# Second mlp of a hybrid block: table rows and layer-norm output transposed in 32x32 blocks by VectorE and placed through DRAM

## The chip, the cores and the metric

The kernel runs on one core of a Trainium2 chip. The metric is the device time of one execution in microseconds (us); a kernel's time is the median of its runs. One execution was also recorded by the hardware profiler. Its span runs from the first to the last recorded event, and line numbers such as L1442 are lines of the kernel before the change.

## The reference

The input is `x`, 4 x 1024 tokens of 256 floats. Four blocks are added one after the other, each on a layer norm of `x`: a state-space block, an mlp with experts, an attention block, and the same mlp with experts once more. The change lies in this last one. With `h` the layer norm of `x`, as rows (all in fp32):

```python
queries = (h @ W_q).reshape(2, n, 64)
routing = einsum('tnd,tdk->tnk', queries, keys)       # 64 scores per half
# the best 8 of each half, their 64 sums, the best 8 of those: 8 indices below 512 (clamped)
ew = silu(einsum('nh,nkh->nk', h, down_embed[indices])) * softmax(scores)
experts = einsum('nk,nkh->nh', ew, up_embed[indices])
x = x + silu(h @ gate_w) * (h @ up_w) @ down_w + experts
```

`reshape(2, n, 64)` makes the scores of one token come from two far apart places, so the scores of a group of tokens need `h` of a group in the first half and of one in the second.

## The kernel before

The 4096 tokens are cut into 8 groups of 512, each held as 4 tiles of 128 tokens. In `ffn` (L1663 on), the second mlp, everything for a group `g` goes this way.

First, for all groups in the order 0, 4, 1, 5, 2, 6, 3, 7 (that of the attention's results), `layernorm` writes ln(x) with tokens on partitions (L111), TensorE transposes it in 128x128 blocks against an identity (`transposed`, L120), and VectorE and ScalarE each copy one half of the result out of PSUM into `hT[g]`, features on partitions (L1681).

Then `route` turns two `hT` into a table: 128 partitions x 4 x 512 floats, `tb`, in which every token has its expert weights at the places of its experts and zero elsewhere. It is a chain of some forty VectorE operations (L1300 to L1435); ScalarE fills in entries (L1360). The scores for table `g` need `hT[g//2]` and `hT[g//2+4]`. The table of group `g+1` is made while group `g` is finished.

For each group in rising order: 8 pairs of gate and up products (`product`, L129) with silu on ScalarE (L1699) and a product on VectorE (`act`, L1701); `chosen` multiplies `hT` by all 512 rows of `down_emb`, takes silu (`wt`, L1454) and weighs it with the table; the scores for the next table; `raise_x` adds down products of `act` and `up_emb` products of `wt` for four tiles, and VectorE adds each to `x` (L1473); `store` writes the group out (L1711).

The table has tokens on partitions and `wt` has experts there, so `spread` has TensorE transpose it, 4 x 4 blocks of 128x128 into `st` in PSUM (L1442), and VectorE multiplies `wt` by each `st` (L1458).

```python
for i in range(4):
    st = self.spread(stp, table, i)
    nc.vector.tensor_tensor(
        wv[:, :, i // 2, :, i % 2], wv[:, :, i // 2, :, i % 2], st, ALU.mult
    )
```

Earlier stages record every operation at L46 and are kept in the order written by hand. In `ffn` the framework's scheduler orders the instructions of each engine when the program is built; that order is fixed in the program. An engine works through its own queue in order, and an instruction that waits holds up all behind it. SP's queue issues nearly all DMAs. The buffers of a pool are reused in turn, and whoever writes one waits for its last reader. DMAs signal on eight semaphores in turn, and each waits for the one that used its semaphore before.

Of the kernel before, what the change touches and what calls it, by code (L numbers as in the profile page):

```python
# [12 lines left out]
F32 = mybir.dt.float32  # L13
AF = mybir.ActivationFunctionType
ALU = mybir.AluOpType
AX = mybir.AxisListType
PSUM = bass.MemoryType.PSUM
DRAM = bass.MemoryType.DRAM

P = 128  # L20
B, L, D = 4, 1024, 256
NT = B * L
KD = D // P
G = 512
NG = NT // G
TG = G // P
# [3 lines left out]
XC = NEXP // P  # L30
# [20 lines left out]
class Net:  # L51
# [1383 lines left out]
        dve.tensor_tensor(tb[:, :, NEXP - 1], tb[:, :, NEXP - 1], last, ALU.add)  # L1435
        got.append(tb)

    def spread(self, pool, tb, i):

        st = pool.tile([P, XC, P], F32, tag="st", name="st")  # L1440
        for c in range(XC):
            self.nc.tensor.transpose(st[:, c, :], tb[:, i, c * P : (c + 1) * P], self.ident)  # L1442
        return st

    def chosen(self, pool, stp, mm, w, h, table):

        nc = self.nc
        wt = pool.tile([P, XC, G], F32, tag="wt", name="wt")
        for c in range(XC):
            ps = self.product(  # L1450
                mm,
                [(w["down_embT"][:, k, c * P : (c + 1) * P], h[:, k, :]) for k in range(KD)],
            )
            nc.scalar.activation(wt[:, c, :], ps, AF.Silu)  # L1454
        wv = wt.rearrange("p c (m j h) -> p c m j h", h=2, j=P)
        for i in range(4):
            st = self.spread(stp, table, i)
            nc.vector.tensor_tensor(  # L1458
                wv[:, :, i // 2, :, i % 2], wv[:, :, i // 2, :, i % 2], st, ALU.mult
            )  # L1460
        return wt

    def raise_x(self, pool, g, w, wt, act):
# [199 lines left out]
    def ffn(self, w, out):  # L1663
        nc, tc = self.nc, self.tc
        with ExitStack() as ctx:
            one = ctx.enter_context(tc.tile_pool(name="ff_one", bufs=1, reuse_waits="tile"))
            two = ctx.enter_context(tc.tile_pool(name="ff_two", bufs=2, reuse_waits="tile"))
            sm = ctx.enter_context(tc.tile_pool(name="ff_sm", bufs=2, reuse_waits="tile"))
            acts = ctx.enter_context(tc.tile_pool(name="ff_act", bufs=IC + 2, reuse_waits="tile"))
            mm = ctx.enter_context(tc.tile_pool(name="ff_mm", bufs=4, space=PSUM, reuse_waits="tile"))  # L1670
            stp = ctx.enter_context(tc.tile_pool(name="ff_st", bufs=2, space=PSUM, reuse_waits="tile"))
            op = ctx.enter_context(tc.tile_pool(name="ff_o", bufs=2, space=PSUM, reuse_waits="tile"))

            hT = [None] * NG
            for g in (0, 4, 1, 5, 2, 6, 3, 7):
                h = one.tile([P, KD, G], F32, tag=f"hT{g}", name=f"hT{g}")
                ln = two.tile([P, TG, D], F32, tag="ln", name="ln")
                self.layernorm(g, ln)
                for k in range(KD):
                    ps = self.transposed(mm, ln, k)  # L1680
                    (nc.scalar.copy if k else nc.vector.tensor_copy)(h[:, k, :], ps)  # L1681
                hT[g] = h

            def route(g):
                got = []
                for _ in self.route(nc, w, g, hT, (one, two, sm, mm), got):
                    pass
                return got[0]

            table = route(0)  # L1690
            for g in range(NG):
                h = hT[g]
                act = []
                for c in range(IC):
                    cs = slice(c * P, (c + 1) * P)
                    pg = self.product(mm, [(w["gate_w"][:, k, cs], h[:, k, :]) for k in range(KD)])
                    pu = self.product(mm, [(w["up_w"][:, k, cs], h[:, k, :]) for k in range(KD)])
                    s = two.tile([P, G], F32, tag="s", name="s")
                    nc.scalar.activation(s, pg, AF.Silu)  # L1699
                    a = acts.tile([P, G], F32, tag="act", name="act")  # L1700
                    nc.vector.tensor_tensor(a, s, pu, ALU.mult)  # L1701
                    act.append(a)
                wt = self.chosen(two, stp, mm, w, h, table)
                if g + 1 < NG:
                    table = route(g + 1)
                self.raise_x(op, g, w, wt, act)
                self.store(out, g)
# [73 lines left out]
```

## Time and profile before

| what | value |
|---|---|
| median of 3 runs | 2012.34 us (2011.7 to 2013.0) |
| profiled execution, its own time | 2012.48 us |
| its span | 2010.8 us, 22729 instructions |
| mean granted clock of TensorE | 0.96 |
| busy: TensorE, VectorE, ScalarE, GpSimd | 89%, 79%, 57%, 44% |
| second mlp: first product L129 with `w_gate_w` | about 1528 us |
| DMA, mean over the span | 48 GB/s; in the second mlp about 10 GB/s |

A busy share is an average over stages with different limits, so the second mlp is read by itself, in stretches that follow its groups. A group line gives line, engine, operation, output<-input, count, busy us and mean ns. SPq lines are the DMA issues on SP's queue; "to landing" is the time from an issue until its completion is signalled.

### The profile page before, as it was taken

The numbers are of one execution on the slowest core, as the hardware profiler recorded it, in microseconds if no ns is written. First come the engines' busy times: TensorE is split into PE (matmuls) and PEld (weight loads), VectorE is DVE, ScalarE is ACT, GpSimd is POOL, SyncE is SP. The second block draws the span as 40 slices with busy tenths as digits, with TensorE's granted clock in tenths as the row PEclk, the third lists the DMA queues.
The fourth block names the chain that finished last, engine by engine and source line by source line (L and its number), as shares of the span: only waits on it lengthen the run. The fifth ranks groups of instructions, "written<-read, shape, count | busy, mean of one in ns | idle before, by whom it ended". The sixth has DMA issues, their size and how long they took to land.

```text
span 2010.8 us, 22729 instructions
## 1 busy us (share of the span) xinstructions
PE 1789.5 (89%) x7450; PEld 1145.2 (57%) x7450; DVE 1592.4 (79%) x2695; ACT 1137.7 (57%) x2315; POOL 894.2 (44%) x612
## 2 busy tenths in 40 slices
PE   8777789889798898898878998899988999999999
PEld 4445446456455564564645656566664666556665
DVE  6999999999999999999999999654457555445551
ACT  5877777867787677776543654745324333233331
POOL 4977888878798797887760000111110000000000
PEclk8868899999999999999899999899998999999999
DMA  4111121221212212212123131010000000000000
GB/s 138 53 33 58 54 73 48 88 73 57 82 56 79 70 53 80 74 59 64 56 81 116 63 100 46 34 63 1 1 1 0 11 11 1 11 11 11 11 11 11
DMA packets 79926, 97.46 MB, mean 48 GB/s; under 512 B 7360, under 2 KB 53312, under 8 KB 79808
## 3 DMA queue, kind: packets, MB, share of 16 engines
q1 hardware_dynamic: 74592, 90.66, 14.6%
q10 hardware_dynamic: 5216, 5.36, 0.8%
q8 instruction: 58, 0.95, 0.2%
q14 instruction: 60, 0.49, 0.1%
HBM read 83.15 MB, written 12.85 MB: 48 GB/s over the span
## 4 chain that ended last, share of the span: by engine, by line
PE 50%; DVE 30%; ACT 11%; issue 8%; POOL 1%; DMA 0%; DVEq 0%; SPq 0%; POOLq 0%; ACTq 0%
PE ps L129 22%; DVE h L46 9%; DVE acc L46 8%; PE hT L46 4%; ACT a L46 3%; PE down L46 3%; PE o L46 2%; PE up L46 2%; PE gate L46 2%; PE skip L46 2%; PE out L46 1%; PE dt L46 1%; PE at L46 1%; ACT xc L46 1%; PE bc L46 1%
## 5 line engine op out<-in xcount | busy, mean ns | idle before, releaser
L46 POOL TENSOR_TENSOR u<-dx,bt 128x1024 f32<-128x1024 f32 x255 | 602.0, 2362 | 140.4 <-DVE h L46 106.0
L46 ACT ACTIVATE a<-delta,a_neg 128x512 f32<-128x512 f32 x512 | 340.9, 687 | 147.9 <-DVE h L46 146.8
L46 PE MATMUL hT<-ident,h 128*128 128x128 f32 x2048 | 317.1, 294 | 120.2 <-DVE acc L46 119.1
L46 PEld LDWEIGHTS hT<-ident,h 128*128 128x128 f32 x2048 | 245.4, 149 | 265.5 <-DVE acc L46 228.4
L46 DVE SCALAR_TENSOR_TENSOR acc<-hT,cT,acc 128x512 f32<-128x512 f32 x512 | 356.8, 740 | 18.0 <-PE hT L46 17.4
L46 DVE TENSOR_TENSOR_SCAN h<-a,state,u 128x512 f32<-128x512 f32 x256 | 317.8, 1285 | 1.3 <-ACT a L46 1.2
L46 DVE TENSOR_TENSOR_SCAN h<-a,u 128x512 f32<-128x512 f32 x256 | 303.9, 1232 | 4.8 <-ACT a L46 2.6
L1701 DVE TENSOR_TENSOR act<-s,ps 128x512 f32<-128x512 f32 x64 | 44.0, 688 | 151.4 <-PE ps L129 151.3
L46 PE MATMUL gate<-hT,gate_w 128*128 128x512 f32 x256 | 124.9, 611 | 14.3 <-ACT acc L46 14.3
L1699 ACT ACTIVATE s<-ps 128x512 f32<-128x512 f32 x64 | 38.1, 596 | 167.4 <-PE ps L129 164.6
L46 PE MATMUL up<-hT,up_w 128*128 128x512 f32 x256 | 122.0, 599 | 2.9 <-DVE xw L46 2.9
L129 PE MATMUL ps<-hT,w_gate_w 128*128 128x512 f32 x256 | 122.1, 600 | 2.5 <-DVE act L1701 2.5
L46 POOL TENSOR_TENSOR xc<-xc,tap 128x512 f32<-128x512 f32 x84 | 110.9, 1320 | 22.8 <-ACT tap L46 22.6
L129 PE MATMUL ps<-hT,w_up_w 128*128 128x512 f32 x256 | 120.3, 592 | 0.0
L46 PE MATMUL down<-w_down_w,av 128*128 128x256 f32 x512 | 118.6, 380 | 1.8 <-DVE xw L46 1.0
L129 PE MATMUL ps<-w_down_w,act 128*128 128x256 f32 x512 | 116.8, 380 | 3.0 <-DVE x L1473 3.0
L129 PEld LDWEIGHTS ps<-w_down_w,act 128*128 128x128 f32 x512 | 96.0, 190 | 21.6 <-DVE x L1473 8.8
L46 PEld LDWEIGHTS down<-w_down_w,av 128*128 128x128 f32 x512 | 94.9, 190 | 20.6 <-issue 8.0
L1360 ACT ACTIVATE tb<-d,ex 128x64 f32<-128x64 f32 x256 | 62.0, 333 | 53.4 <-DVE ex L1350 48.4
L46 ACT ACT_TABLE_LOAD x63 | 80.8, 1283 | 17.7 <-DMA w_wd2T<-in_wd2T 8.8
L46 PE MATMUL out<-w_out_wT,y 128*128 128x256 f32 x256 | 68.3, 414 | 18.6 <-DVE y L46 18.4
L129 PEld LDWEIGHTS ps<-hT,w_gate_w 128*128 128x128 f32 x256 | 48.9, 192 | 60.4 <-issue 56.0
(296 smaller groups left out, 3079.0 us busy)
## 6 DMA issues: line engine op xcount, KB each, us to landing
bt<-bcd SPq DMA_DIRECT2D x127, 256.0 KB, 3.2
gate_w<-in_gate_w SPq DMA_DIRECT2D x64, 128.0 KB, 2.5
up_w<-in_up_w SPq DMA_DIRECT2D x64, 128.0 KB, 2.2
in_wT<-in_in_wT SPq DMA_DIRECT2D x8, 512.0 KB, 3.8
hs<-hT SPq DMA_DIRECT2D x8, 512.0 KB, 2.9
xs<-xw SPq DMA_DIRECT2D x8, 512.0 KB, 2.8
hT<-hs SPq DMA_DIRECT2D x8, 512.0 KB, 4.5
x<-xs SPq DMA_DIRECT2D x8, 512.0 KB, 4.6
```

Source lines behind the costliest of these rows:

```text
L46: return self.tc.keep_in_program_order(f(*args, **kw))
L129: self.nc.tensor.matmul(ps, lhsT=lhsT, rhs=rhs, start=i == 0, stop=i == len(pairs) - 1)
L1360: nc.scalar.activation(tbv[:, m, i, :], d[:, M4 + m, 0:NKEY], AF.Copy, scale=ex[:, m, i : i + 1],)
L1699: nc.scalar.activation(s, pg, AF.Silu)
L1701: nc.vector.tensor_tensor(a, s, pu, ALU.mult)
```

## The change

In `ffn` neither the table nor ln(x) goes through TensorE any more. `turned` has VectorE transpose each tile in 32x32 blocks (128 partitions in four quarters of 32, each block within its quarter) into an SBUF tile, and SP stores that tile to DRAM in one DMA. What is then still in the wrong place is put right by loads from DRAM. For the table, `spread` issues 16 loads of 64 KB (runs of 512 B) into `rows`, one for each quarter of the partitions and each 128 experts. For ln(x), 32 loads of 16 KB (runs of 128 B) go into `hT[g]`, one for each quarter, feature half and tile. `wt` is then multiplied by `rows` in SBUF. The PSUM pool of `spread` is gone and the pool `mm` has 6 buffers instead of 4; the table has one buffer instead of two, and `spread` is called right after `route`.

```diff
-    def spread(self, pool, tb, i):
-
-        st = pool.tile([P, XC, P], F32, tag="st", name="st")
-        for c in range(XC):
-            self.nc.tensor.transpose(st[:, c, :], tb[:, i, c * P : (c + 1) * P], self.ident)
-        return st
-
-    def chosen(self, pool, stp, mm, w, h, table):
+    def turned(self, pool, dram, src, name):
+
+
+        n = src.shape[2]
+        out = pool.tile([P, n // 32, TG, 32], F32, tag=name, name=name)
+        for t in range(TG):
+            self.nc.vector.transpose(
+                out[:, :, t, :], src[:, t, :].rearrange("p (b j) -> p b j", j=32)
+            )
+        d = dram.tile([P, n // 32, TG, 32], F32, tag=name, name=name)
+        self.nc.sync.dma_start(out=d, in_=out)
+        return d
+
+    def spread(self, pool, dram, tb):
+
+        d = self.turned(pool, dram, tb, "tbt")
+        rows = pool.tile([P, XC, P // 32, TG, 32], F32, tag="rows", name="rows")
+        for q in range(P // 32):
+            for c in range(XC):
+                self.nc.sync.dma_start(
+                    out=rows[q * 32 : (q + 1) * 32, c],
+                    in_=d[:, 4 * c + q, :, :].rearrange("(a i) t j -> i a t j", i=32),
+                )
+        return rows
+
+    def chosen(self, pool, mm, w, h, rows):
...
-        wv = wt.rearrange("p c (m j h) -> p c m j h", h=2, j=P)
+        wv = wt.rearrange("p c (m a j h) -> p c m a j h", h=2, j=32, a=P // 32)
         for i in range(4):
-            st = self.spread(stp, table, i)
-            nc.vector.tensor_tensor(
-                wv[:, :, i // 2, :, i % 2], wv[:, :, i // 2, :, i % 2], st, ALU.mult
-            )
+            part = wv[:, :, i // 2, :, :, i % 2]
+            nc.vector.tensor_tensor(part, part, rows[:, :, :, i, :], ALU.mult)
         return wt
...
-            mm = ctx.enter_context(tc.tile_pool(name="ff_mm", bufs=4, space=PSUM, reuse_waits="tile"))
-            stp = ctx.enter_context(tc.tile_pool(name="ff_st", bufs=2, space=PSUM, reuse_waits="tile"))
+            mm = ctx.enter_context(tc.tile_pool(name="ff_mm", bufs=6, space=PSUM, reuse_waits="tile"))
+            dram = ctx.enter_context(tc.tile_pool(name="ff_dram", bufs=2, space=DRAM))
...
-                for k in range(KD):
-                    ps = self.transposed(mm, ln, k)
-                    (nc.scalar.copy if k else nc.vector.tensor_copy)(h[:, k, :], ps)
+                d = self.turned(one, dram, ln, "lnt")
+                for q in range(P // 32):
+                    for k in range(KD):
+                        for t in range(TG):
+                            nc.sync.dma_start(
+                                out=h[q * 32 : (q + 1) * 32, k, t * P : (t + 1) * P].rearrange(
+                                    "i (a j) -> i a j", j=32
+                                ),
+                                in_=d[:, 4 * k + q, t, :].rearrange("(a i) j -> i a j", i=32),
+                            )
                 hT[g] = h
...
-                for _ in self.route(nc, w, g, hT, (one, two, sm, mm), got):
+                for _ in self.route(nc, w, g, hT, (one, one, sm, mm), got):
                     pass
-                return got[0]
+                return self.spread(one, dram, got[0])
```

More of the change, by code (lines that the diff above doesn't have):

```diff
@@ L1702, in ffn @@
                     act.append(a)
-                wt = self.chosen(two, stp, mm, w, h, table)
+                wt = self.chosen(two, mm, w, h, table)
                 if g + 1 < NG:
```

## The prediction

> **What bounds the kernel now.** I read the busy times by stage first, then the chain of work that ended last, the waits, and last the DMA issues on SP. The change sits in the second mlp, from about 1500 us to the end (columns: window, its length, then busy time and count of PE, PEld, DVE, ACT, POOL; TensorE's granted clock; DMA share; GB/s):
>
> ```profile
> 1500.00:1528.00 28.00, 20.18 (x111) 16.10 (x110) 21.77 (x73) 5.76 (x10) 4.03 (x4) 0.82 0.00 1
> 1567.00:1627.00 60.00, 59.56 (x211) 36.52 (x210) 29.50 (x71) 19.64 (x50) 0.00 (x0) 1.00 0.03 10
> 1627.00:1686.00 59.00, 58.58 (x205) 36.33 (x204) 29.68 (x71) 18.34 (x48) 0.00 (x0) 1.00 0.03 10
> ```
>
> In the seven later groups TensorE is busy 99% of the time and VectorE half. In the opening 28 us TensorE waits for layer norms. The chain (start, us, what) gives one round:
>
> ```profile
> 1626.55 0.87 PE st L1442 x8
> 1627.42 0.67 PE route L1276 x6
> 1628.09 1.12 PE st L1442 x8
> 1629.21 1.13 PE route L1276 x10
> ...
> 1642.83 43.24 PE ps L129 x124
> 1686.08 0.87 PE st L1442 x8
> ```
>
> A round is 1686.08 - 1626.55 = 59.5 us, and the 16 `st` transposes take 0.87 + 1.12 = 1.99 us of it, on the path. SP does nothing in this stage but store results:
>
> ```profile
> 1596.14 410.95 SPq L1711 DMA_DIRECT2D out_x<-x  x8
> ```
>
> It will now issue some 400 DMAs. What one issue costs (ns min/median/max) stands in earlier stages:
>
> ```profile
> L46 SPq DMA_DIRECT2D x<-xs x8: 338/432/459, 1064.9 to 1258.3; - x8
> L46 SPq DMA_DIRECT2D hT<-hs x8: 319/449/938, 1064.3 to 1256.1; - x8
> L46 SPq DMA_DIRECT2D keys<-in_keys x4: 535/648/705, 33.4 to 35.5; - x4
> ```
>
> The shortest are single issues after a wait; those in a row are the 432 to 475 ns ones, and 42 to 45 ns lie between two of them.
>
> **What is taken away.** Per group, 16 transposes of table rows: 1.99 us x 8 = 15.9 us of TensorE on the path. For ln(x), 64 transposes (12.0 us of TensorE beside a VectorE chain) and 16 copies, 8 of them 0.69 us on VectorE.
>
> **What VectorE gets.** Four block transposes of 128x512 per table. No block transpose is in the trace; the nearest row is a 128x512 fp32 operation, 0.69 us, so 2.8 us per group (ends: half of it, were two elements a cycle possible, and 5.0 by the page below). VectorE has 29 us free in a round and the table is not due at once, so I charge nothing; without that cover it would be 22 us over eight groups. For ln(x), four of 128x256 per group at 0.41 us, less than the copy removed plus the wait for TensorE. Here a rule speaks against the change. The Trainium skill's "VectorE: DVE Perf Modes", The three transpose paths, gives 311 ns for VectorE's 128x128 bf16 transpose (in 32x32 blocks only) and 390 ns for TensorE's, and its rules send 128x128 to TensorE. In this trace TensorE's cadence is 0.87/8 = 0.11 us, so the step saves 2.0 us a group and not 6.2 as by the page; on VectorE the page would make the table 16 x 0.311 = 5.0 us and my row 2.8. Either is hidden.
>
> **What SP gets, group by group.** The instruction order of the changed program decides this. SP's queue is: store lnt(0), 32 loads into hT(0), then the same for groups 4, 1, 5; store lnt(2), store tbt(0), 32 loads hT(2); store lnt(6), 3 loads of rows(0), 32 loads hT(6); store lnt(3), 3 of rows(0), 32 of hT(3); store lnt(7), 3 of rows(0), 32 of hT(7); the last 7 of rows(0). So the first group's rows stand behind all eight ln(x), 272 loads in all. Each first load waits for its store to land, so SP stands still for it and all behind it waits too.
>
> One load is 16 KB in 128 packets of 128 B. What does it cost? Three candidates:
> - SP's issue: 0.43 to 0.475 + 0.044 us between = 0.48 us.
> - The DMA engines: in the window from 1 to 4 us the ACT queue moved 473 packets (4 to 16 B) in 11.6% of 16 engines, 0.116 x 16 x 3 / 473 = 12 ns each. 144 packets on 16 engines are then 0.11 us. Not the limit.
> - Landing: a load waits for the one eight before it (eight semaphores in turn). Small ones land in 1.6 us (`bcd`, 32 KB) to 2.5 us (`w_conv_w`, 512 packets); 2.2/8 = 0.28 us. Not the limit.
>
> So 0.48 us. Ends: 0.36 us (319 + 42, as if each were a single issue) and 0.69 us (`keys`, issued in a row while the DMA engines were 70 to 90% busy). The row of `x<-xs`, loads from DRAM in a row, is the nearest.
>
> This is where the second rule counts. "DMA: Bandwidth & Descriptors", Issuing engines are not separate DMA queues, says that the sequencer's time to initiate a DMA is usually small relative to the DMA itself. By it, 32 loads would cost what one 512 KB load does (`hT<-hs`, 4.5 us), and by the row 32 x 0.48 = 15.4 us. By the rule the rows land in time and the change gains; by the row they are late. I go by the row.
>
> Sum. VectorE comes to the first lnt when it has added the last attention output (1507.2 in the trace of before) and 4 x 0.34 us at the cadence of 128x256 operations: store at 1508.4. A 512 KB store lands in 2.9 us (`hs<-hT`, `out_x<-x`), 3.1 with hand-over: 8 x 3.1 = 24.8, less 4.6 us of issues (3 x 3 loads of rows and the tbt store) that pass under those waits: 20.2. Loads: 272 x 0.48 = 130.6. Last landing 2.2. rows(0) complete: 1508.4 + 20.2 + 130.6 + 2.2 = 1661.4.
>
> When does TensorE want them? hT(0) lands at 1508.4 + 3.1 + 15.4 + 2.2 = 1529.1, and group 0's gate/up pairs begin there (1528.0 before, but then with the routing scores done). A pair takes 3.43 us, the spacing of `act` in the timeline of before. hT(4), needed for the scores, lands at 1547.6, five pairs (17.2) later: a stop of 1 us. Three more pairs, scores and the expert product (10.3 + 1.8 + 6.9) end near 1567, the next scores and the down products of two tiles (1.8 + 6.9) near 1575. Six pairs of group 1 run ahead (20.6 us; hT(1) landed at 1566): 1596. Then nothing is left: the next instruction takes `wt`, weighed with rows(0). VectorE's own queue is also stopped there, with the x updates and group 1's further `act` behind the weighing.
>
> TensorE stands from 1596 to 1661.4 + 4 x 0.69 + 0.1 = 1664.3. After it: the up_emb products of two tiles (3.4), the two other tiles (10.3), two gate/up pairs (6.9), the expert product (6.9) = 27.5. Group 1's expert product ends at 1691.8; before, at 1626.5. **+65.3 us.** From there groups 1 to 7 save 7 x 1.99 = 13.9. The granted clock falls where TensorE waits (0.82 in the opening window above): I add 2 us for a restart. Net +53.4 on a span of 2010.8, 2064.2; with the 1.7 us around the span (the profiled execution took 2012.48, the median of the runs is 2012.34, so nothing to shift) **2066 us**.
>
> **Costed at nothing.** Later rounds: the table is complete 25.9 us after the expert product (1652.4 - 1626.5). Four transposes 2.8, a 1 MB store 5 (`w_gate_w`, 1 MB load, 4.8), 16 loads 7.7, landing 2.2, hand-overs 0.4: 44 of 57.5 us, 14 us to spare; at 0.69 us still 10. Were that gone, each microsecond of lateness would cost seven. Weighing from SBUF: a 128x512 operation with SBUF sources (L1305) takes 692 ns, from PSUM 686. It may follow the expert product by 0.6 + 2.8 us while TensorE has 1.8 of scores and 3.4 of down products: hidden by 1.8 us. PSUM from 4 to 6 buffers: between 0 and -6 us (waits of TensorE for `act`, 2.5 + 3.3); I take 0, since these fall before the standstill. The one table buffer is free 25 us before it is refilled. The out_x stores are queued behind rows, but the last rows land about 20 us before the end.
>
> **Rivals.**
> 1. As above, SP's issue: 2066; at 0.36 us SP outruns VectorE (route(0)'s 25 us and route(1)'s stand ahead of lnt(2), tbt(0), lnt(3) and lnt(7)), rows(0) come at about 1638 instead of 1629, and the time is about 2042. Against it: no row has more than five issues in a row.
> 2. Not slower: small DMAs overlap as the rule says and an issue is almost free. All transfers hide, TensorE keeps only the gain of 15.9: about 1997. The turning point is rows(0) at 1610 (delay 13.9), an issue of 0.29 us by my sum. For it: 12 ns packets. Against: no SP issue in the trace is under 317 ns.
> 3. Backed up like `keys`: 0.69 us, rows(0) at 1718, 2123. For it: the `keys` are the smallest rows in a train. Against: the DMA engines would here be about a quarter busy.
> 4. The change does what it says in later rounds but rows are late there too (44 us would have to pass 57.5: an issue over 1.3 us): then rows(0) come near 1885 and the time is 2290 or more.
>
> **Chances.** First 0.70, third 0.18, fourth 0.04, second 0.05, between the turning point and 0.36 us 0.03. Range 2036 to 2118: from 0.36 us, slightly below, to just short of the third. Within 0.2% (4 us, about what a measurement can tell from no change): 0.02; faster 0.05; slower 0.93.
>
> **What would show it.** SP's hT issues at 0.48 us each and unbroken from 1511 to about 1660; DMA share low meanwhile; one standstill of TensorE of about 68 us released by DVE's weighing, which waits for `rows`; then rounds of 57.5 us with no wait for rows. If issues take 0.25 us, or the hole comes once per round, I am wrong.

## The result and the profile after

The changed kernel takes 2063.84 us (median of 4 runs, 2063.65 to 2064.2) against 2012.38 us for the kernel before beside it (4 runs, 2011.7 to 2013.0). The ratio is 1.0255, 95% interval 1.0239 to 1.027: slower by 51.5 us. The profiled execution took 2064.2 us, its span 2062.5 us.

The second mlp by windows, after (the columns are those of the prediction's first fence):

```profile
1500.00:1528.00 28.00, 9.28 (x37) 6.74 (x36) 14.38 (x57) 2.36 (x3) 4.03 (x4) 0.68 0.17 37
1600.00:1660.00 60.00, 3.27 (x4) 0.67 (x2) 9.41 (x15) 0.00 (x0) 0.00 (x0) 0.53 0.32 71
1700.00:1758.00 58.00, 57.81 (x197) 35.77 (x196) 32.40 (x76) 18.76 (x48) 0.00 (x0) 1.00 0.14 46
```

The middle row is the loss. For 60 us all four engines do next to nothing, and the DMA engines are busy a third of the time, so no engine and no bandwidth is the limit there. The last row is a later round: TensorE is full again.

What SP did meanwhile is in its timeline after (start us, us from the first to the end of the last issue, number of issues):

```profile
1509.58 0.32 SPq L1448 DMA_DIRECT2D lnt<-lnt  x1
1512.34 15.04 SPq L1699 DMA_DIRECT2D hT<-lnt  x32
1527.47 0.38 SPq L1448 DMA_DIRECT2D lnt<-lnt  x1
1530.27 15.01 SPq L1699 DMA_DIRECT2D hT<-lnt  x32
...
1638.15 1.81 SPq L1457 DMA_DIRECT2D rows<-tbt  x3
1640.63 15.01 SPq L1699 DMA_DIRECT2D hT<-lnt  x32
1655.68 3.28 SPq L1457 DMA_DIRECT2D rows<-tbt  x7
```

32 loads take 15.0 us, one after the other, eight times. The last 7 loads of the first group's rows come when everything else is through. One row sums up all 256 loads, in ns min/median/max:

```profile
L1699 SPq DMA_DIRECT2D hT<-lnt x256: 302/430/1418, 1512.3 to 1655.2; - x128
```

With the gap to the next one, 15.01 / 32 = 0.47 us per load. Who waits for that is in the waits of the stretch from 1500 us on (total, times, longest):

```profile
ACT s L1722 <- DVE act L1724: 76.3, 1, 76.3
...
PE ps L129 <- DVE wt L1476: 59.4, 1, 59.4
...
DVE wt L1476 <- DMA rows<-tbt: 37.4, 1, 37.4
```

It is one wait passed along. VectorE's weighing waits for `rows`; TensorE waits for the weighing; and ScalarE, which has run ahead, waits for `act` products that stand behind the weighing in VectorE's queue. VectorE's wait reads shorter than TensorE's because VectorE is first busy with the table of group 1 until 1608 us, and then stands 14.3 us for the one `lnt` buffer, which is free only when its store, itself late in SP's queue, has landed. TensorE's timeline shows both ends of the gap:

```profile
1599.49 3.78 PE L129 MATMUL ps<-hT,w_up_w 128*128 128x512 f32 x4 [1.65 <-ACT s L1722]
1662.67 6.61 PE L129 MATMUL ps<-w_up_emb,wt 128*128 128x256 f32 x16 [59.40 <-DVE wt L1476]
1669.12 3.62 PE L129 MATMUL ps<-w_down_w,act 128*128 128x256 f32 x16
```

The first 16 products after the gap take 6.61 us, the next 16 of the same size 3.62. The granted clock is 0.50 in every stretch of the trace from the restart to 1668.1 us and 1.00 from 1668.6 us on: TensorE works at half speed for about 5.5 us.

### The profile page after: what moved, and what is told of

It reads as the page before. It is cut to its first block, busy times and chain, and to the rows that moved or that the text cites. A ratio compares the mean times of both kernels' runs of the same rounds, so it can differ in the third digit from the quotient of the medians.

```text
span 2062.5 us, 22883 instructions
## 1 busy us (share of the span) xinstructions
PE 1770.4 (86%) x7258; PEld 1127.7 (55%) x7258; DVE 1615.2 (78%) x2751; ACT 1133.0 (55%) x2307; POOL 894.3 (43%) x612
## 4 chain that ended last, share of the span: by engine, by line
PE 46%; DVE 31%; ACT 10%; issue 8%; SPq 3%; DMA 1%; POOL 1%; DVEq 0%; ACTq 0%; POOLq 0%
PE ps L129 21%; DVE h L46 8%; DVE acc L46 8%; PE hT L46 3%; PE down L46 3%; ACT a L46 3%; SPq L1699 3%; PE o L46 2%; PE up L46 2%; PE skip L46 2%; PE gate L46 2%; PE out L46 2%; PE dt L46 1%; PE at L46 1%; ACT xc L46 1%
## 5 line engine op out<-in xcount | busy, mean ns | idle before, releaser
L1722 ACT ACTIVATE s<-ps 128x512 f32<-128x512 f32 x64 | 38.1, 597 | 262.6 <-PE ps L129 186.3
L46 PE MATMUL gate<-hT,gate_w 128*128 128x512 f32 x256 | 123.3, 604 | 14.3 <-ACT acc L46 14.3
L129 PE MATMUL ps<-w_up_emb,wt 128*128 128x256 f32 x256 | 63.3, 392 | 59.4 <-DVE wt L1476 59.4
L129 PEld LDWEIGHTS ps<-w_up_emb,wt 128*128 128x128 f32 x256 | 50.2, 197 | 68.8 <-DVE wt L1476 61.7
```

Of the source, the lines that this page charges most:

```text
L46: return self.tc.keep_in_program_order(f(*args, **kw))
L129: self.nc.tensor.matmul(ps, lhsT=lhsT, rhs=rhs, start=i == 0, stop=i == len(pairs) - 1)
```

## The experiments

My theory was that of the prediction: SP's time per issue, 272 loads in one queue up to and with the first group's last rows. The rivals: A, that the 128-B packets or their landing take the time, however few DMAs carry them; B, that VectorE's chain of norms and routing would hold the rows back anyway; C, that TensorE's gain is not real. All of these kernels compute the whole reference. Each comparison with the kernel before is with its runs on the same chip, whose medians were 2010.8, 2012.5 and 2012.1 us. The full change was not run again beside them, so a difference from its 2063.8 us carries the 2 us by which these medians differ.

**Twice the issues, the same packets** (full change).

```diff
+    for a in range(0, P // 32, 2):
+        c0 = t * P + a * 32
         nc.sync.dma_start(
-            out=h[q * 32 : (q + 1) * 32, k, t * P : (t + 1) * P].rearrange(
+            out=h[q * 32 : (q + 1) * 32, k, c0 : c0 + 64].rearrange(
...
-            in_=d[:, 4 * k + q, t, :].rearrange("(a i) j -> i a j", i=32),
+            in_=d[a * 32 : (a + 2) * 32, 4 * k + q, t, :].rearrange(
```

> The full change, but each of the 256 hT loads is two loads of half the blocks (8 KB, 64 packets): bytes and 128-B packets are the same, issues ahead of rows(0) grow by 256. Theory (SP's time per issue, 0.474 us between two in a row): rows(0) come 256 x 0.474 = 121 us later, near 1783 us, all of it in one standstill of TensorE in front of group 0's down products: about 2185 us (2165 to 2190). Rival A (packets set the time): 2064 us, no change from the full change. Rival B (VectorE's chain): about 2064 to 2080 us.

Measured: 2181.5 us (ratio 1.0849, 1.0833 to 1.0865), 117.7 us more than the full change (119.3 by the losses against the kernel before). Its issue row and its SP timeline:

```profile
L1701 SPq DMA_DIRECT2D hT<-lnt x512: 302/425/1813, 1511.9 to 1774.5; - x171
```

```profile
1511.93 29.92 SPq L1701 DMA_DIRECT2D hT<-lnt  x64
```

Half the bytes and half the packets in a load, and the issue takes the same 0.43 us (29.92 / 64 = 0.47 with the gap). The bytes and packets in all are the same, and the time grows as the count of issues says (256 x 0.47 = 120); rival A is out.

**Few issues, the same packets** (full change). Four stores put ln(x)'s blocks in order, in 4096 runs of 128 B, and four loads of 2 KB runs fill `hT`.

```diff
-                d = self.turned(one, dram, ln, "lnt")
...
+                d = dram.tile([32, D // 32, TG, P // 32, 32], F32, tag="lnt", name="lnt")
+                for a in range(P // 32):
+                    nc.sync.dma_start(
+                        out=d[:, :, :, a, :].rearrange("i b t j -> i (b t) j"),
+                        in_=lnt[a * 32 : (a + 1) * 32].rearrange("i b t j -> i (b t) j"),
+                    )
                 for q in range(P // 32):
...
+                    nc.sync.dma_start(
+                        out=h[q * 32 : (q + 1) * 32],
+                        in_=d.rearrange("i (k q) t a j -> i k q (t a j)", q=P // 32)[:, :, q, :],
+                    )
```

> The full change, but ln(x)'s blocks are put in order by four stores of 32 partitions in runs of 128 B, and hT is filled by four loads of 2 KB runs: 8 DMAs for a group instead of 33, with as many 128-B packets as before, now on the store's side. Theory (SP's time per issue): SP is held 8 x 0.47 = 3.8 us a group and no longer 15.1 + 0.3; a group's transfer takes about 9 us from first store to last landing, rows(0) is there near 1585 us, before TensorE's 1596, the standstill of 59 us is gone and 7 to 8 x 2.2 us of TensorE stay gained: about 1998 us (1990 to 2010). Rival A (the 128-B packets and their landing are what takes the time): 4096 packets a group still take some 15 us, the standstill stays: about 2060 us. Rival B (VectorE's own chain, the single lnt buffer and the routing ahead of lnt(2), lnt(3) and the table, sets when rows(0) are there): rows(0) come no earlier than about 1630 us, and the time is about 2035 us.

Measured: 2029.6 us (ratio 1.0091, 1.0076 to 1.0106). My number was wrong: 33 to 34 us of the loss are gone, not all of it. A group's transfer took 10.8 us (first store 1507.2, last landing 1518.0) where I had said 9, so this is not rival A. It is rival B, in a form I had put only into a side sentence of the prediction. SP's timeline:

```profile
1579.91 2.49 SPq L1707 DMA_DIRECT2D hT<-lnt  x4
1595.73 3.03 SPq L1702 DMA_DIRECT2D lnt<-lnt  x4
1598.81 2.14 SPq L1457 DMA_DIRECT2D rows<-tbt  x3
...
1620.33 2.01 SPq L1457 DMA_DIRECT2D rows<-tbt  x4
```

and its waits:

```profile
SPq L1702 <- DVE eq L1399: 15.7, 1, 15.7
SPq L1448 <- DVE tbt L1444: 11.5, 1, 11.5
```

SP now idles. The two waits are those ahead of the store of lnt(5) and of table 0 (each named by the VectorE operation that ended last before it); a third, of 13 us, is the gap ahead of lnt(6) in the timeline. The loads of rows(0) stand in its queue behind the stores of lnt(6), lnt(3) and lnt(7). The transposes for lnt(6) stand in VectorE's queue behind the whole routing for group 1 and its table's transposes, and are done only at 1595.7 us, although table 0 was stored at 1568.1. lnt(3) and lnt(7) follow through the one `lnt` buffer. The standstill of TensorE is still 30.9 us.

**The rows in another queue** (full change with its 256 loads of `hT`).

```diff
-                self.nc.sync.dma_start(
+                self.nc.gpsimd.dma_start(
                     out=rows[q * 32 : (q + 1) * 32, c],
```

> The full change with its 256 hT loads on SP as they are, but the loads of rows are issued by GpSimd, which has nothing else to do in this stage. SP still needs until about 1645 us for its queue. Theory (what costs is that rows(0) stands behind all eight ln(x) in one queue): rows(0) then waits only for the table's store at 1582 to 1586 us and for 16 issues of an engine whose price in a train no run has shown (0.5 to 1 us each), so it is there at 1596 to 1604 us; the standstill shrinks from 59 to at most 10 us: about 2003 us (1993 to 2015). Rival A (the hT transfers themselves are slow or hold up the DMA engines, whatever queue the rows are in): rows land near 1650 us, about 2050 us. Rival B (VectorE's order, in which lnt(3) and lnt(7) stood ahead of group 0's weighing and wait for their single buffer): the weighing comes at about 1640 us, about 2040 us.

Measured: 2007.3 us (ratio 0.997, 0.9958 to 0.9982). GpSimd's and TensorE's timelines:

```profile
1587.37 8.93 POOL L1457 DMA_DIRECT2D rows<-tbt  x16 [71.33 <-DMA hT<-lnt]
```

```profile
1606.85 6.38 PE L129 MATMUL ps<-w_up_emb,wt 128*128 128x256 f32 x16 [4.95 <-DVE wt L1476]
```

The standstill shrinks from 59.4 to 4.95 us, while SP still issues its loads at 0.47 us, until 1660 us. So it is not the sum of the work that costs, but that rows(0) stood at the end of it. Nor do the `hT` transfers hold up the DMA engines: the first group's rows, issued among them, land 2.5 us after their issue (median; 2.1 in the full change). The scheduler also moved group 0's weighing ahead of lnt(3) and lnt(7) on VectorE, so this run doesn't separate the two queues. The Trainium skill's "DMA: Bandwidth & Descriptors", Issuing engines are not separate DMA queues, says that several issuing engines save only the sequencer's time, which is usually small. Here it is not: in the full change SP spends 62 us on `hT` loads between the store of table 0 and the last of its rows, and this run is 56 us faster (VectorE's new order may have a part in it).

**The first table moved up in the program** (full change).

```diff
             for g in (0, 4, 1, 5, 2, 6, 3, 7):
+                if g == 1:
+                    table = route(0)
...
-            table = route(0)
```

> The full change with the call of the first group's routing and table moved up in the program, behind the ln(x) of groups 0 and 4; the planner then puts all 16 loads of rows(0) behind 112 hT loads instead of 272, but those of rows(1) still stand behind all 256. The number of SP's issues is unchanged. Theory: rows(0) are there at about 1590 us, before TensorE runs dry, and the standstill there is gone; rows(1) cannot come before SP is through, about 1672 us as in the full change, and TensorE, which can run ahead by six pairs of group 2, stands for about 20 to 25 us in group 1 instead: about 2015 us (2005 to 2025). Rival A (the hT transfers hold up all DMAs): 2050 us or more. Rival B (VectorE's chain of norms and routing, not the queue): 2040 us or more, or a standstill still in group 0.

Measured: 2027.4 us (ratio 1.007, 1.0055 to 1.0085). TensorE's timeline:

```profile
1597.78 2.08 PE L129 MATMUL ps<-hT,w_up_w 128*128 128x512 f32 x2 [4.75 <-ACT s L1723]
...
1683.33 5.96 PE L129 MATMUL ps<-w_up_emb,wt 128*128 128x256 f32 x16 [24.55 <-DVE wt L1476]
```

As expected, the hole moves from group 0 to group 1, whose last rows now stand at the end of SP's queue (SP is through at 1680 us, not the 1672 that I took from the full change). The time is above my range, 12 us above my number. As the standstill ends with those rows, 8 of the 12 are SP's: it stood 4.3 us for table 0 and 7.9 us for table 1, which VectorE had not yet transposed. The restart at half clock took 2.3 more; the rest I did not place. That TensorE came late to the standstill (group 1's expert product begins at 1622.5 us, 10 us after that of the table half below) only made the standstill shorter.

**The two halves alone.** The table by VectorE and DRAM with ln(x) by TensorE as before:

```diff
-                d = self.turned(one, dram, ln, "lnt")
...
+                for k in range(KD):
+                    ps = self.transposed(mm, ln, k)
+                    (nc.scalar.copy if k else nc.vector.tensor_copy)(h[:, k, :], ps)
```

> Only the table half of the change: the expert rows go by VectorE's block transposes, one store and 16 loads through DRAM, while ln(x) is transposed by TensorE and copied as in the kernel before. Theory: SP has 16 issues and a store in its queue ahead of the weighing of group 0, so rows(0) come at about 18 us after the table (2.8 + 4 + 7.6 + 2), near 1580 us; no standstill above 10 us; each round saves TensorE 2.2 us: about 1998 us (1993 to 2006). Rival B (the table's way by VectorE and DRAM is itself late in every round, because the transposes or the store stand behind other work): rounds of 60 us or more with a wait for rows in each, 2015 us or more. Rival C (TensorE's gain is not real, its rounds were shortened by something that followed the standstill): rounds of 59.5 us, about 2012 us.

And the other way round, ln(x) by VectorE and DRAM, the table by TensorE as before (with its four buffers in `mm`):

```diff
+                d = self.turned(one, dram, ln, "lnt")
...
-                for k in range(KD):
-                    ps = self.transposed(mm, ln, k)
-                    (nc.scalar.copy if k else nc.vector.tensor_copy)(h[:, k, :], ps)
```

> Only the ln(x) half: ln(x) by VectorE's block transposes, a store and 32 loads a group; the expert rows are transposed by TensorE as before. Theory: SP is held as long as in the full change (until about 1640 us), but no row of a table stands behind it; what is late is only hT(4), at 1547 us, and with it group 0's scores and table: a loss of 5 to 15 us in the first round, none in the others and no gain in any: about 2020 us (2014 to 2028). Rival B (the ln(x) half alone costs what the full change costs, for instance because VectorE's transposes and their waits hold up its other work): about 2050 us or more.

Measured: the table half 1990.9 us (ratio 0.9903, 0.9888 to 0.9918), and 1990.0 (0.9893, 0.988 to 0.9907) when measured again beside a later version. The ln(x) half 2017.1 us (1.0028, 1.0018 to 1.0039). (The traced execution of the latter, 2012.1 us, was the fastest of its eight and shows 3 of the 6 us: its opening is 4.7 us shorter than in the kernel before, from the last attention product to group 0's expert product, and from there to group 1's it takes 65.6 us instead of 57.8, as `hT` and the first table come late. The later rounds are as before.) The table half's time lies below the range that I gave. One half gains 20 to 22 us and the other loses 6; together they should gain some 15 us, and they lose 51. What costs is neither half but that the table's rows wait behind ln(x)'s transfers in SP's queue. SP's timeline of the table half:

```profile
1552.24 0.32 SPq L1448 DMA_DIRECT2D tbt<-tbt  x1
1556.14 7.46 SPq L1457 DMA_DIRECT2D rows<-tbt  x16
```

Nothing stands ahead of rows(0), and they are issued by 1563.6 us. Its expert products begin every 57.30 us, those of the kernel before every 59.52 (first two lines: table half; last two: before):

```profile
1612.39 7.03 PE L129 MATMUL ps<-hT,w_down_embT 128*128 128x512 f32 x16
1669.69 7.03 PE L129 MATMUL ps<-hT,w_down_embT 128*128 128x512 f32 x16
1619.52 7.03 PE L129 MATMUL ps<-hT,w_down_embT 128*128 128x512 f32 x16
1679.05 7.03 PE L129 MATMUL ps<-hT,w_down_embT 128*128 128x512 f32 x16
```

Rival C is out: 2.2 us a round are real. Of these, 1.99 are the transposes; the rest is TensorE's wait for the update of `x`, 0.4 us in a round before and 0.2 now.

**VectorE's transposes twice** (table half).

```diff
-        for t in range(TG):
+        for t in (*range(TG), *range(TG)):
             self.nc.vector.transpose(
```

> The table half alone, with each of VectorE's four block transposes of the table done twice in a row into the same tile (the second changes nothing): 4 x 0.67 = 2.7 us more of VectorE a group, and the table's store 2.7 us later. Theory (VectorE's part is hidden, the rows have some 10 us or more to spare in every round): 1991 us as without it (1988 to 1995). Rival (VectorE's work or the table's way is on the path): 8 x 2.7 = 21 us more, 2012 us.

Measured: 1993.4 us (ratio 0.99, 0.9885 to 0.9914). The rounds stay at 57.30 us to the hundredth; its profiled execution is longer than that of the table half only by what lies ahead of its first expert product (1561.3 against 1556.5 us; from there to the end 431.7 against 432.0). So 19 us more of VectorE's transposes (38.9 instead of 19.9) cost nothing.

**Four PSUM buffers** (table half): `bufs=6` of `mm` set to `bufs=4`.

> The table half alone, with four PSUM buffers for products instead of six. The table half came out 20 us faster than the kernel before where 8 x 2.2 = 17.6 us of transposes are gone; in its trace group 0's expert product begins at 1556.5 us instead of 1561.7. If two more PSUM buffers let TensorE run further ahead of ScalarE and VectorE in the opening, four give back 3 to 6 us, with waits of TensorE for act in the first 60 us as before: about 1995 us. If they are worth nothing: 1991 us, and the rest of the gain is elsewhere.

Measured: 1994.3 us (ratio 0.9902, 0.9885 to 0.9918), which the runs don't tell apart from six. The traces do. From the last transposes of ln(x) that had to wait for VectorE to group 0's expert product it takes 38.1 us with four buffers and 38.2 in the kernel before, 34.8 us with six (both in the table half and with the doubled transposes). With four, a stop is back that the kernel before has at the same place:

```profile
1544.18 3.61 PE L129 MATMUL ps<-hT,w_gate_w 128*128 128x512 f32 x4 [2.46 <-DVE act L1717]
```

Two more buffers are thus worth 3.3 us in the opening and nothing later. With them the table half's gain adds up, as an estimate: 15.9 us of transposes, 1.5 of shorter waits for `x` and 3.3 make 20.7.

**Both cures at once**: few DMAs for ln(x) on SP, rows on GpSimd; the diffs are those above.

> Both cures at once: ln(x) by four stores and four loads a group on SP, and the loads of rows on GpSimd. Theory: the table's store comes at about 1568 us as it did with few DMAs, so rows(0) take 1572 + 16 x 0.55 (GpSimd's measured time per issue) + 2.3 = 1584 us, before TensorE runs dry; no standstill above 5 us; the opening is about 5 us shorter than with ln(x) by TensorE, the rounds are 57.3 us: about 1987 us (1982 to 1997), level with or a little under the table half alone. Rival B (VectorE's order and the single lnt buffer hold the weighing of group 0 behind lnt(6) or later, whatever the queues do): a standstill of 10 to 30 us, 2005 us or more.

Measured: 1998.7 us (ratio 0.9934, 0.992 to 0.9947). No wait of TensorE's products for the weighing above 0.2 us is left (its weight loads wait 1.1 us at most), so the cause of the loss is fully taken away. But it is 9 us slower than the table half beside it, and my 1987 was wrong, as was its range. Group 1's expert product begins at 1618.0 us instead of 1612.4 (5.6 of the 6.0 us between the two profiled spans), after stops of TensorE for VectorE and ScalarE of 0.3, 2.6, 1.7 and 2.6 us, most of them followed by products at a lower clock. VectorE is busy for 70 of the 92 us from 1505 on in both versions: TensorE, fed earlier, waits for it there instead. The table half, measured again beside it, is the fastest version found:

> The table half alone, measured again beside the version above: 1991 us (1988 to 1995).

## Why the prediction was right

| step | predicted | measured |
|---|---|---|
| one hT load on SP, with gap | 0.48 us | 0.47 |
| SP from the first store: hT loads | 256 x 0.48 = 122.9 | 122.2 |
| the loads of rows(0) | 16 x 0.48 = 7.7 | 8.7 |
| stores and what they wait for | 20.2 | 18.5 |
| rows(0) complete | 1661.4 | 1660.9 |
| TensorE starts again | 1664.3 | 1662.7 |
| group 1's expert product ends, against before | +65.3 | +66.8 (1693.2 - 1626.4) |
| rest of the span, against before | -13.9 | -15.1 |
| clock at the restart | +2 | +3.0, within the +66.8 |

By the whole, 2066 was predicted and 2063.8 measured. The last line but one is the later rounds: 57.30 us instead of 59.52, 2.22 saved in each and not 1.99. The spans differ by 66.8 - 15.1 = 51.7 us.

The mechanism is the one forecast, but that rows(0) came within 0.5 us of the sum is in part luck: the first store was 1.2 us late and the loads of `rows` took 1.0 us more, while the stores took 1.7 and the `hT` loads 0.7 less.

- *The price of an issue.* 0.48 us from `x<-xs` held, and with it the choice against the page. An issue (0.43 us) is in fact small beside its own DMA, which lands after 1.7 us. The point is that DMAs overlap and the issues of one queue don't: 32 loads take 32 issues and one landing. The rule is true of one DMA and misleads for a train of small ones. The other end, 0.69 us, fell to the doubling: trains of 64 loads kept 0.47.
- *The standstill.* Its end was right within 2 us. Its start was 7 us late (1603.3 instead of 1596), because TensorE's last pairs waited 4.0 and 1.7 us and ran at a lower clock. That cost nothing, as what ended the standstill was rows(0).
- *The clock.* I had charged 2 us. The first 16 products after the gap lost 6.61 - 3.62 = 3.0 us; after the gaps of the other versions 2.1 (doubled issues, 5.74), 2.3 (first table moved up, 5.96) and 3.3 (few issues, 6.87). The granted clock stays at 0.50 for about 5.5, 3.7, 4.2 and 6.0 us in these four. The Trainium skill's "TensorE: Matmul & The Clock Gate", What's actually happening, has the first 3.4 us or so of work at half rate and all after it at full rate; an estimate from that is a loss of 1.7 us. All four traces show a longer stretch. The same section says that the window of 3.4 us in which the work is watched runs free. If one whole window must be busy, an estimate is 3.4 to 6.8 us at half rate, and the four lie in it; no run here tests that reading.
- *VectorE hidden.* The 128x512 block transpose takes 0.67 us and the 128x256 one 0.40 (I took 0.69 and 0.41); the four of a table take 2.5 us together, not the 5.0 worked out from the page. The doubling shows that this work is free, as said.
- *Later rounds.* The table's rows are issued by 1733.0 us and land 2.1 us later, 16 us before the weighing at 1751.3 (14 predicted); no wait for rows is in any of these rounds.
- *PSUM at 0.* Right for this change, where the opening ends in the standstill. In the table half, where there is none, it is 3.3 us, inside the 0 to 6 that I gave. The 6 was too wide: the 2.5 and 3.3 us that I added are one and the same stop at 1541 us, seen by the product and by its weight load.
- *The second rival was mis-figured.* I gave 1997 us for issues that are almost free, and a turning point at 0.29 us per issue. With 8 issues in place of 33 the time was 2029.6 us. Below some 0.36 us VectorE's queue takes over, as the first rival's side sentence has it (rows(0) near 1629 to 1638 and 2042 us; measured with few issues: rows landed at 1624.1, 2029.6). I had worked that out for one rival and left it out of the next: as this order puts rows(0) behind lnt(7), even free issues would hardly do. An estimate from the few-issues trace: lnt(6) ready at 1595.7, three stores of 2.9 us (as `out_x` took before; 2.8 for `lnt` in the full change) one behind the other with two transposes of 1.4 between them, the rows' landing of 2.2 give 1609.4 instead of 1624.1, so about 2015 us and not 1997. No run tried it. What does bring a gain is another queue for the rows (2007.3) or leaving ln(x) on TensorE (1990).

Left open: the 5.6 us that the version with both cures loses in group 0. I read them as TensorE's stops behind VectorE and ScalarE, but took none of them away by itself. How much VectorE's order alone and SP's order alone hold back the rows in the run with rows on GpSimd isn't separated either.

## What to carry to other kernels

Before moving work to many small DMAs, count the issues and write down the queue: (issues ahead of the transfer that is needed first) x (time of one issue in a row) is a time, even when bytes and packets are few and the DMA engines two thirds idle, as here. Then do the same for the engine that feeds that queue: an early transfer that stands behind a late one waits for all that the late one waits for. And test the parts of a change alone; here one half was worth 20 us, and the other buried it.

## What the runs showed of the hardware

- SP's time per issue hardly depended on size up to 64 KB: median 0.425 us for 8 KB, 0.430 for 16 KB and for the 64 KB of `rows`; 0.59 for a 128-KB load and 0.68 for a 128-KB store in 1024 runs of 128 B.
- GpSimd issued the same 64-KB loads of `rows` at 0.55 us each, trains of 16 in 8.7 to 8.9 us, against 7.4 to 9.0 us on SP. I had allowed up to 1 us.
- A 128x512 fp32 block transpose on VectorE took 0.67 us, as other 128x512 fp32 operations did here (0.67 to 0.69).
- After a standstill TensorE was granted half its clock for 3.7 to 6.0 us, a loss of 2.1 to 3.3 us.
